# Products of blocks by sevens for queries, gates and outputs, in a hybrid of attention, feed-forward and state layers

## The chip, the cores and the metric

The kernel runs on one core of a Trainium2 chip. Times are device microseconds (us) of one execution. The engines are TensorE (PE: matmuls, with weight loads as PEld beside them), VectorE (DVE), ScalarE (ACT) and GpSimd (POOL), and SyncE (SP), whose queue issues nearly all DMAs. All data is f32.

## What is computed

Four layers stand one behind the other on a stream x of 4 batches, 1024 tokens and 256 features; each adds to x. The same feed-forward layer is used twice.

```
x = x + attention(layernorm(x))
x = x + ffn(layernorm(x))
x = x + state(layernorm(x))
x = x + ffn(layernorm(x))
```

Attention is causal, with one head of 256: Q, K and V are products of 256x256 weights with a bias. The feed-forward layer mixes each token with the one before it, and gives sigmoid(xr Wr) * (relu(xk Wk)^2 Wv). The state layer is, in the reference's words:

```python
xn = (x - mu) / jnp.sqrt(var + 1e-05) * ln_g + ln_b
xz = xn @ W_in.T + b_in
x_proj, z = jnp.split(xz, 2, axis=-1)
z = jax.nn.silu(z)
...
y = x_mean @ W_C.T + D_skip * x_proj
y = y * z
y = y @ W_out.T + b_out
return y + residual
```

Between these lines, x_proj is reduced to 16 states, and each state is convolved over time with its own decay. Three products matter here: the queries (in the kernel one product of xn with a merged weight wm, since Q and K are folded into one), the gates z, and the outputs y @ W_out.

## The kernel before

**Tiles.** The kernel works by halves j of a batch: 512 tokens (HALF) by 256 features. Activations are kept with features on the partitions, as two chunks c of 128 features by 512 tokens, or with tokens on the partitions, as four rows of 128 tokens by 256 features. The stream x stays on the core, tokens on the partitions. A product with features on the partitions is `project_columns` (L653 on): for one chunk e of 128 output features, two matmuls (c = 0, 1) of 128 x 512 that accumulate in one PSUM bank. A product with tokens on the partitions is `project_rows` (L667 on): for two rows of tokens, four matmuls of 128 x 256 into one bank, the tokens' columns as stationary weights. A matmul in f32 is two instructions on TensorE.

- `queries(j, e)` (L1163): `project_columns` of xa with wm, then one copy with the bias from PSUM, on ScalarE or VectorE.
- `state_gates(j, e)` (L1394): `project_columns` of xnT with the second half of w_in, then SiLU with the bias from PSUM on ScalarE.
- `state_outputs(j, g)` (L1570): `project_rows` of the gated z with w_out, then one VectorE add of 128 x 512 to x (L1577).

So each batch (two halves) has eight matmuls of 512 columns for queries, eight for gates, and sixteen of 256 columns for outputs.

**Memory.** All working tiles of the phases come from one pool of 34 equal slots. A new tile takes a slot that an older one has left, and its first writer waits until that one's last reader is done. PSUM has four single banks ("bank") and two pairs of banks ("pair"); scores and `skip` take pairs, the other products banks.

**Order.** The class `Order` (L49 on) records every step: a unit of TensorE with its cost, or an operation of another engine with one or more ways to do it (engine, cost), its needs, and what PSUM it frees. TensorE's units run in the order in which they were written down. `finish` (L162) works out by when each operation is due, and then goes through time with these costs: each engine takes the operation that can start first, and of those the one that is due first. What it chooses is written out as the fixed instruction order of each engine. `columns` (L41) is the cost of a unit's matmuls, `SHARE` and `MARGIN` (L65) say how much of its slack an operation may be held back.

**Phases.** The loop at L1627 is the attention phase: 32 score units (one for 128 queries), with the queries, values and feed-forward units of earlier halves between them (`mix_units`, L1590). After L1662 comes the last phase: the feed-forward units of halves 6 and 7, the gates, the reduction to states (`state_inputs`), the decay tables' loads (`load_decay`, sixteen DMAs of 512 KB, L1467), four convolutions (`convolve`, L1478), the exchange of their results through DRAM (`states_out`, L1498: four writes, L1503; `states_in`, L1515: four reads a batch, L1520), `skip(j)` (L1527: the product D_skip * x_proj, eight matmul instructions of 512 columns into a pair), `mix_states(b)` (L1541: it adds the states' part to the pairs of both halves, and VectorE gates z with them, L1556, four instructions a batch), the outputs, and `mix2`, the second feed-forward layer. `mix2.prepare(j)` makes a half's inputs: statistics on VectorE (L526, L527), a power on GpSimd (L543), normalization (L558, L564), a write and four reads through DRAM that turn it (L604, L610, with L616 on VectorE), and the mixture with the token before (L712 on ScalarE, L715 on VectorE). The feed-forward result is multiplied by its gate on VectorE (L791) and added to x on GpSimd (L797).

## Time and profile before

| | |
|---|---|
| median of three runs | 472.55 us (471.34, 472.55, 472.76) |
| the profiled execution | 471.39 us, its span 469.2 us |
| TensorE busy | 463.4 us (99%), 2074 matmul instructions |
| VectorE busy | 335.0 us (71%) |
| ScalarE busy | 190.6 us (41%) |
| GpSimd busy | 110.0 us (23%) |
| granted TensorE clock | 1.00 |
| moved by DMA | 69.42 MB, mean 148 GB/s |

The span runs from the first instruction of the program to the last; the execution's own time has some 2 us around it. A group's row in the profile names the line, the engine and the operation, then out<-in tiles and shapes, the count, the busy time and the mean of one in ns. A wait's row gives the total, the number of times and the longest. "SPq" rows are DMA issues; their durations are those of the issue, not of the transfer. A timeline row gives the start and the length of a run of equal instructions.

### The profile page before, as it was taken

The page shows a single profiled execution, that of the slowest core. Times are in us where ns is not written, and L with a number is a line of the kernel's source. Part 1 is how long each engine was busy: PE and PEld are TensorE (multiplying, and loading weights), DVE is VectorE, ACT ScalarE, POOL GpSimd, SP SyncE. Part 2 cuts the span into 40 slices and gives each one's busy share as a digit, 9 for nine tenths or more (in the row PEclk, how much of TensorE's full clock was granted, in tenths as well). Part 3 has the DMA queues.
Part 4 walks back from the last instruction along what each step waited for, and adds up shares of the span by engine and source line. Part 5 has one row for each costly group of instructions (what it writes and reads, how often), then busy time and mean ns, then how long its engine had stood idle before and what let it go on. Part 6 is the DMA issues. An engine that isn't in the chain of part 4 may idle for free.

```text
span 469.2 us, 6471 instructions
## 1 busy us (share of the span) xinstructions
PE 463.4 (99%) x2074; PEld 317.2 (68%) x2074; DVE 335.0 (71%) x886; ACT 190.6 (41%) x348; POOL 110.0 (23%) x119
## 2 busy tenths in 40 slices
PE   8999999999999999999999999999999999999996
PEld 5765775857867757866768756474565875877765
DVE  3678879589898897786897985411577984986642
ACT  3521333335235534537442585501113454345632
POOL 3000301112402503503322374300001310243330
PEclk9999999999999999999999999999999999999999
DMA  7047864844647854628883588903032241425312
GB/s 233 26 121 216 264 174 104 243 128 143 196 115 144 228 152 136 161 77 247 258 253 88 175 270 229 342 1 80 11 113 90 80 145 45 133 92 179 92 67 67
DMA packets 84914, 69.42 MB, mean 148 GB/s; under 512 B 20161, under 2 KB 82577, under 8 KB 84881
## 3 DMA queue, kind: packets, MB, share of 16 engines
q1 hardware_dynamic: 84064, 68.76, 49.7%
q8 instruction: 16, 0.26, 0.2%
q10 hardware_dynamic: 816, 0.26, 0.2%
q14 instruction: 18, 0.14, 0.1%
HBM read 40.54 MB, written 28.45 MB: 147 GB/s over the span
## 4 chain that ended last, share of the span: by engine, by line
PE 96%; DMA 1%; DVE 1%; ACT 0%; SPq 0%; issue 0%; DVEq 0%
PE sc L1217 13%; PE po L1322 13%; PE py L1534 6%; PE pv L1189 6%; PE pc L1484 2%; PE py L1546 1%; DMA wq<-in_L_attn_a_Wq_dram 1%; PE pb L1421 1%; PE pp_a0.pq L659 1%; PE pr_g1.pv L674 1%; PE pr_g0.pr L674 1%; PE pr_f4.pr L674 1%; PE pr_f3.pr L674 1%; PE pr_f2.pr L674 1%; PE pr_f1.pr L674 1%; PE pr_f0.pr L674 1%
## 5 line engine op out<-in xcount | busy, mean ns | idle before, releaser
L1322 PE MATMUL po<-v,prT 128*128 128x256 f32 x288 | 67.9, 380 | 0.4 <-DVE prT L1275 0.3
L1217 PE MATMUL sc<-xa,q 128*128 128x512 f32 (+3 forms) x192 | 67.0, 486 | 0.0
L1322 PEld LDWEIGHTS po<-v,prT 128*128 128x128 f32 x288 | 54.2, 190 | 11.1 <-issue 2.4
L1217 PEld LDWEIGHTS sc<-xa,q 128*128 128x128 f32 x192 | 35.2, 190 | 23.6 <-issue 18.7
L1238 ACT ACTIVATE pr<-pr,nmx 128x128 f32<-128x128 f32 (+7 forms) x32 | 24.7, 772 | 57.7 <-DVE pr L1233 55.5
L1189 PE MATMUL pv<-wv,xa 128*128 128x257 f32 x128 | 32.9, 380 | 0.0
L797 POOL TENSOR_TENSOR x<-x,r_g 128x512 f32<-128x512 f32 x14 | 20.1, 1432 | 51.7 <-DVE r_g L791 41.3
L543 POOL TENSOR_TENSOR rs_f<-ve_f,minus_half 128x4 f32<-128x4 f32 x8 | 8.3, 1037 | 99.3 <-DVE ve_f L530 99.3
L797 POOL TENSOR_TENSOR x<-x,r_f 128x512 f32<-128x512 f32 x16 | 20.3, 1271 | 42.9 <-DVE r_f L791 41.7
L1189 PEld LDWEIGHTS pv<-wv,xa 128*128 128x128 f32 x128 | 24.1, 191 | 7.8 <-issue 2.9
L1534 PE MATMUL py<-xnT,wk 128*128 128x512 f32 x64 | 28.8, 596 | 0.0
L1233 DVE TENSOR_SCALAR_CACHE_REDUCE pr<-sc,v 128x128 f32<-128x128 f32 (+7 forms) x32 | 26.2, 818 | 1.1
L1556 DVE SCALAR_TENSOR_TENSOR z<-py,b_skip,z 128x512 f32<-128x512 f32 x16 | 11.0, 742 | 22.2 <-PE py L1546 22.2
L1275 DVE STREAM_TRANSPOSE prT<-pblocks 128x384 f32<-128x384 f32 (+7 forms) x30 | 23.9, 797 | 3.2 <-DMA pblocks<-exps 3.0
L1332 DVE SCALAR_TENSOR_TENSOR x<-po,rsm,x 128x256 f32<-128x256 f32 x32 | 15.5, 484 | 12.4 <-PE po L1322 10.2
L543 POOL TENSOR_TENSOR rs_g<-ve_g,minus_half 128x4 f32<-128x4 f32 x8 | 8.6, 1078 | 58.3 <-DVE ve_g L530 55.8
L1366 POOL TENSOR_TENSOR x<-x,bout_r 128x512 f32<-128x512 f32 x16 | 20.4, 1286 | 8.1 <-ACT x L1359 8.0
L1534 PEld LDWEIGHTS py<-xnT,wk 128*128 128x128 f32 x64 | 12.0, 190 | 13.7 <-issue 13.0
L543 POOL TENSOR_TENSOR rs_h<-ve_h,minus_half 128x8 f32<-128x8 f32 x8 | 13.8, 1720 | 30.0 <-DVE ve_h L532 27.3
L1359 ACT ACTIVATE x<-x,mrs_h,rs 128x256 f32<-128x256 f32 x32 | 17.2, 590 | 2.9 <-DVE rsm L1331 2.9
L1199 DVE TENSOR_TENSOR v<-pv,bv_r 128x257 f32<-128x257 f32 x32 | 13.2, 414 | 6.9 <-PE pv L1189 6.6
L712 ACT ACTIVATE xk_g<-hT_g,muk 128x512 f32<-128x512 f32 x16 | 11.1, 715 | 16.6 <-DVE hT_g L616 16.6
(429 smaller groups left out, 949.9 us busy)
## 6 DMA issues: line engine op xcount, KB each, us to landing
hk<-r_dram SPq DMA_DIRECT2D x16, 512.0 KB, 8.3
rows_g<-xn_g SPq DMA_DIRECT2D x8, 512.0 KB, 3.1
blocks_g<-rows_g SPq DMA_DIRECT2D x32, 128.0 KB, 2.7
x<-in_L_attn_a_X_dram SPq DMA_DIRECT2D x7, 512.0 KB, 4.9
rows_f<-xn_f SPq DMA_DIRECT2D x7, 512.0 KB, 3.4
blocks_f<-rows_f SPq DMA_DIRECT2D x28, 128.0 KB, 2.8
rows_h<-xn_h SPq DMA_DIRECT2D x7, 512.0 KB
blocks_h<-rows_h SPq DMA_DIRECT2D x28, 128.0 KB, 3.5
```

The costliest lines, as they stand in the source:

```text
L543: nc.gpsimd.tensor_tensor(rs()[:, :k].rearrange("p k n -> p (k n)"), ve()[:, :k].rearrange("p k n -> p (k n)"), minus_half[:, : k * NH], A ...
L674: nc.tensor.matmul(pr()[:, j, :], lhsT=src()[:, c, ts(2 * g + j, P)], rhs=w[:, c, :], start=(c == 0), stop=(c == KC - 1),)
L797: nc.gpsimd.tensor_add(xg, xg, r()[:, ts(g, 2), :])
L1189: nc.tensor.matmul(pv()[:, : D + 1], lhsT=xaj()[:, c, ts(n, P)], rhs=wv[:, c, :], start=(c == 0), stop=(c == KC - 1),)
L1217: nc.tensor.matmul(sc()[:, k * HALF : k * HALF + w], lhsT=qh()[:, c, ts(n, P)], rhs=keys[k]()[:, c, :w], start=(c == 0), stop=(c == KC - 1),)
L1233: nc.vector.tensor_scalar(dst, src, v[2 * b + h]()[:, n, D : D + 1], None, ALU.add, ALU.min, accum_out=nmx(),)
L1238: nc.scalar.activation(p()[:, :nk], p()[:, :nk], AF.Exp, bias=nmx(), scale=-1.0, accum_out=sm())
L1275: nc.vector.transpose(dst()[:, : NH * width].rearrange("p (k m a) -> p k m a", m=NH, a=GRP), blocks().rearrange("p m (k a) -> p k m a", a= ...
L1322: nc.tensor.matmul(po()[:, :D], lhsT=src()[:, ts(n, P)], rhs=v[2 * b + n // NH]()[:, n % NH, :D], start=(n == 0), stop=(n == t),)
L1359: nc.scalar.activation(xt, xt, AF.Identity, bias=mrs()[:, 0, n : n + 1], scale=rs1()[:, n : n + 1])
L1366: nc.gpsimd.tensor_add(xg, xg, bout_r.unsqueeze(1).to_broadcast([P, 2, D]))
L1534: nc.tensor.matmul(dst()[:, ts(e, HALF)], lhsT=w_x[:, c, ts(e, P)], rhs=src()[:, c, :], start=(c == 0), stop=False,)
```

## The change

Queries of batches 2 and 3, gates of batches 1 to 3 and outputs of all four batches are computed for a whole batch at once, as a product of 2 x 2 blocks in seven products in place of eight (Winograd's form). The weight's blocks a(e, c) are 128 x 128; the stream's blocks b(c, h) are 128 features by the 512 tokens of half h. Four sums of weight blocks are made once on VectorE (`weight_sums`), four sums of stream blocks a batch on GpSimd or VectorE (`stream_sums`, tiles T0 and T1). Each of the seven products has a bank of its own, and its result is added by parts, mostly on VectorE. One scratch tile u is carried along. For gates, SiLU comes after that, on the tile itself.

For outputs (`seven_rows`) tokens are on the partitions: a product is four matmuls of 128 x 128. There are two scratch tiles, u and w. What belongs to one block alone is added from PSUM to x on VectorE, and the shared parts u and w on GpSimd (`grow`).

```diff
-    return 2 * k * max(n * 0.845e-3, 0.19)
+    return 2 * k * max(n * 0.845e-3, 0.105)
...
+    def weight_sums(t, a):
+        nc.vector.tensor_add(t[:, 0], a(1, 0), a(1, 1))
+        nc.vector.tensor_sub(t[:, 1], t[:, 0], a(0, 0))
+        nc.vector.tensor_sub(t[:, 2], a(0, 0), a(1, 0))
+        nc.vector.tensor_sub(t[:, 3], a(0, 1), t[:, 1])
...
+    def stream_sums(key, src, needs):
...
+        for k, plus, minus in (
+            (1, lambda: b(0, 1), lambda: b(0, 0)),
+            (3, lambda: b(1, 1), lambda: b(0, 1)),
+            (2, lambda: b(1, 1), lambda: sums(1)),
+            (4, lambda: b(1, 0), lambda: sums(2)),
+        ):
...
+                ("POOL", 1.05, partial(emit, nc.gpsimd)), ("DVE", dve(HALF), partial(emit, nc.vector)),
...
+    def seven_products(key, sums_key, a, s_of, src, t_of, out, bias, needs, there):
...
+        p = unit(1, lambda: a(0, 0), lambda: src(0)[:, 0, :], there)
+        o.op(f"{key}.u1", [f"{key}.p1"], *copies(u, p), frees="bank")
+        yield
+        p = unit(2, lambda: a(0, 1), lambda: src(0)[:, 1, :], there)
+        add("c11", 2, p, u, block(0, 0), 0, ["u1"])
+        yield
+        p = unit(6, lambda: s_of(2), lambda: t_of(2), [f"{sums_key}.T2"])
+        add("u2", 6, p, u, block(0, 1), None, ["u1"])
+        yield
+        p = unit(7, lambda: s_of(3), lambda: t_of(3), [f"{sums_key}.T3"])
+        add("u3", 7, p, block(0, 1), u, None, ["u2", "c11"])
+        yield
+        p = unit(4, lambda: a(1, 1), lambda: t_of(4), [f"{sums_key}.T4"])
+        add("c21", 4, p, u, block(1, 0), 1, ["u3"])
+        yield
+        p = unit(5, lambda: s_of(1), lambda: t_of(1), [f"{sums_key}.T1"])
+        add("c22", 5, p, u, block(1, 1), 1, ["u3"], last=False)
+        add("v12", 5, p, block(0, 1), block(0, 1), 0, ["u3"])
+        yield
+        p = unit(3, lambda: s_of(4), lambda: src(1)[:, 1, :], there)
+        add("c12", 3, p, block(0, 1), block(0, 1), None, ["v12"])
...
+    def seven_rows(key, sums_key, a, s_of, src, t_of, block, grown, needs, there):
...
+                for n in range(NH):
+                    nc.tensor.matmul(
+                        p()[:, n, :], lhsT=data()[:, ts(n, P)], rhs=wt(), start=True, stop=True
+                    )
...
+        def grow(name, e, h, more, need):
...
+                ("POOL", 1.3, lambda: nc.gpsimd.tensor_add(block(e, h), block(e, h), more())),
...
+        p = unit(2, lambda: a(0, 1), lambda: src(0)[:, 1, :], there)
+        add("v11", 2, p, to(0, 0), to(0, 0), grown(0))
+        grow("x11", 0, 0, u, k("u1", "v11"))
...
+        p = unit(5, lambda: s_of(1), lambda: t_of(1), [f"{sums_key}.T1"])
+        add("v22", 5, p, to(1, 1), to(1, 1), grown(1), last=False)
+        grow("x22", 1, 1, u, k("u3", "v22"))
+        add("w2", 5, p, w, w, k("u3", "v22"))
+        yield
+        p = unit(3, lambda: s_of(4), lambda: src(1)[:, 1, :], there)
+        add("w3", 3, p, w, w, k("w2"))
+        grow("x12", 0, 1, w, k("w3"))
```

The planner changes too. `finish` goes through time for 20 plans (five pairs of `SHARE` and `MARGIN`, four values of a new `WAIT`: an operation that is due sooner may be taken if it can start within `WAIT` of the first), and writes out the one whose end by its own costs is soonest. In the attention phase the queries' products are put one at a time between other units (`go_on`, at least 0.8 us of other units apart), the feed-forward units come two score units later, and two halves' inputs are prepared four score units sooner. The order of the last phase is new around the outputs:

```diff
-        j, k = divmod(i - 8, 4) if i < NI - 1 else (6, 0)
+        j, k = divmod(i - 10, 4)
...
     skip(1)
+    more_gates(4)
+    mix_states(0)
+    more_gates(4)
+    outputs = outputs_of_batch(0)
+    advance(outputs, 2)
+    skip(2)
+    advance(outputs, 2)
+    skip(3)
+    advance(outputs, 3)
+    prepare_batch(0)
+    mix_states(1)
     more_gates(3)
-    mix_states(0)
+    skip(4)
+    outputs = outputs_of_batch(1)
+    advance(outputs, 2)
+    skip(5)
+    advance(outputs, 5)
+    prepare_batch(1)
+    mix_states(2)
     more_gates(2)
-    outputs(0)
-    skip(2)
-    skip(3)
-    mix_states(1)
-    outputs(1)
-    outputs(2)
-    skip(4)
-    outputs(3)
-    skip(5)
     both(mix2.keys, 0)
-    mix_states(2)
     both(mix2.gates, 0)
+    outputs = outputs_of_batch(2)
+    advance(outputs, 2)
     both(mix2.values, 0)
-    outputs(4)
+    advance(outputs, 2)
     both(mix2.keys, 1)
-    outputs(5)
+    advance(outputs, 3)
+    prepare_batch(2)
     both(mix2.gates, 1)
     skip(6)
+    more_gates(2)
     both(mix2.keys, 2)
     skip(7)
     mix_states(3)
     both(mix2.values, 1)
-    outputs(6)
+    outputs = outputs_of_batch(3)
+    advance(outputs, 2)
     both(mix2.gates, 2)
-    outputs(7)
+    advance(outputs, 3)
     both(mix2.values, 2)
+    advance(outputs, 2)
+    prepare_batch(3)
```

There, `more_gates(n)` takes the next n gate units: whole matmul pairs for batch 0, and one of the seven products each for batches 1 to 3. `advance(outputs, n)` does n of the seven products of the outputs. `mix2.prepare` of both halves now follows the whole batch's outputs.

## Prediction

> **What bounds the kernel now.** I read the page's busy times and slices first, then TensorE's waits, then the costs of one matmul by shape, then the timeline of the exchange in the last phase. The page:
>
> ```profile
> span 469.2 us, 6471 instructions
> ...
> PE 463.4 (99%) x2074; PEld 317.2 (68%) x2074; DVE 335.0 (71%) x886; ACT 190.6 (41%) x348; POOL 110.0 (23%) x119
> ...
> DVE  3678879589898897786897985411577984986642
> ...
> PE 96%; DMA 1%; DVE 1%; ACT 0%; SPq 0%; issue 0%; DVEq 0%
> ```
>
> TensorE is busy 99% of the span, and the chain that ended last is 96% TensorE. A busy TensorE is not yet a TensorE without holes, so its own waits come next (us in total, times, longest):
>
> ```profile
> PE dust L1034 <- DVE idle L353: 1.2, 1, 1.2
> PE po L1322 <- DVE prT L1275: 0.3, 1, 0.3
> PE pt_wq_n L1045 <- DMA wq<-in_L_attn_a_Wq_dram: 0.2, 1, 0.2
> ```
>
> These are all of them: 1.7 us, nearly all before the first real matmul. So every matmul that goes is worth its full spacing, and every wait that the change makes is paid in full. VectorE is the second engine: in the slices it stands mostly at 7 to 9 tenths through the attention phase (90 to 290 us: 167.8 of 200 us busy), at 4, 1 and 1 tenths from 293 to 328 us, at 4 to 9 after that, and falls off at the end.
>
> **What one matmul costs.** The mean of one (592, 379, 275 ns) includes a tail of about 165 ns that the next one covers; the spacing is read from starts:
>
> ```profile
> 322.31 1.88 PE L659 MATMUL pp_pz0.6_2930<-xnT,w_in 128*128 128x512 f32 x4
> 324.02 1.88 PE L659 MATMUL pp_pz1.6_2939<-xnT,w_in 128*128 128x512 f32 x4
> ...
> 330.44 1.89 PE L674 MATMUL pr_pyo0.0_2966<-w_out,z 128*128 128x256 f32 x8
> 332.17 1.89 PE L674 MATMUL pr_pyo1.0_2971<-w_out,z 128*128 128x256 f32 x8
> ```
>
> An f32 matmul is two instructions ("passes"). Four passes of 512 columns take 324.02 - 322.31 = 1.71 us, 0.429 each; eight of 256 take 1.73, 0.216 each. For 128 columns with fresh weights each time, the last rows of the program:
>
> ```profile
> 463.90 1.49 PE L818 MATMUL pr_g7.last<-w_fv,ka_g 128*128 128x256 f32 x10
> 464.12 1.08 PEld L818 LDWEIGHTS pr_g7.last<-w_fv,ka_g 128*128 128x128 f32 x8
> ```
>
> The window holds two passes of 256 and eight of 128 columns: 1.49 - 0.165 - 2 x 0.216 = 0.893, so 0.112 each. Eight loads of 190 ns stand within 1.08 us: they start 0.13 apart and lie beside the matmuls.
>
> **The change, step by step.**
>
> *TensorE.* A batch's queries or gates are 8 matmuls of 512 columns before, 7 after: 2 x 0.429 = 0.86 us less. Queries change in two batches, gates in three: 5 x 0.86 = 4.3. Outputs are 32 passes of 256 columns a batch (6.91 us) and become 28 matmuls, 56 passes of 128 columns (6.27): 0.64 x 4 = 2.6. In the built programs' orders TensorE goes from 1088 to 1131 instructions, 48 - 5 more, which is this and nothing else. **Sum: -6.85 us.**
>
> The outputs' part hangs on the 128-column spacing. The row above says 0.112. [...] The row shows full-height loads beside matmuls, so I keep 0.112.
>
> *The exchange of states.* The convolutions' result goes to DRAM and back before the first product with it (mix_states(0), L1546):
>
> ```profile
> 317.05 3.70 PE L1534 MATMUL py<-xnT,wk 128*128 128x512 f32 x8
> ...
> 317.51 1.78 SPq L1503 DMA_DIRECT2D m_dram<-xm  x4
> ...
> 320.75 7.72 SPq L1520 DMA_DIRECT2D xmT<-m_dram  x12
> ...
> 325.83 1.14 PE L1546 MATMUL py<-xmT,w_c 16*128 16x512 f32 x8
> ```
>
> Twelve reads take 7.72 us to issue, so the fourth (the last of batch 0) goes out at 322.7; a read lands 2.6 us after its issue (2.6 to 3.5 over sixteen): 325.3. The cover is skip(1), 8 passes, and three gates, 12 passes: 8.6 us from 317.05, just enough. After, it is skip(1) and four single products, 16 passes: 6.86 us, TensorE ready at 323.9. **+1.4 us**; 0.5 if the writes land sooner, 2.3 with a landing of 3.5.
>
> *Decay tables and the slots.* The new tiles (two sums and one or two scratch tiles a batch) come from the same 34 slots. In the built program the load of hk_2_0, last of sixteen, gets the slot of xnT_0, whose last reader is skip(0); before, no load there reuses a slot freed less than some 14 us of matmuls earlier. From the end of skip(0) to convolve(2), which needs it, TensorE has four transposes (0.45), two products (1.72) and two convolutions (7.20 / 4 = 1.8 each): 5.8 us. These loads land 4.8 to 9.1 us after issue, median 8.3; plus 0.4 of issue that is 0.6 early at one end, 3.7 late at the other. The slow landings stand in the stretch where eight were issued in 4.69 us; this one goes out alone, so I take the short one: **0**, bounds 0 and +3.7.
>
> *VectorE.* An add of a product out of PSUM is L1577's instruction, 0.60 from start to start. Queries: 14 adds and 5 stream sums in two batches, against 8 copies of which ScalarE has most; some +10 us in 200 with 168 busy: 90%. I went along the two orders and compared, from each VectorE instruction that reads a product to each TensorE instruction that waits for VectorE, the work of both. In the kernel before, no stretch has more VectorE work than TensorE work. After, the attention phase's tightest is 21.4 against 21.6 us: **0**, bound +1.5. In 310 to 430 us VectorE has 78 us now and gets 28 adds of outputs less the 16 that go, 15 of gates and 10 sums and copies: 37 x 0.60 = 22, so 100 in 116. One place overflows: after mix_states(1) TensorE has three products (2.57 us) before skip(4), which needs the PSUM pair that two of L1556's instructions (0.66 each) free, and between these VectorE's order has three pairs of statistics (0.53 each) and a small one: 3.0 + 0.2 for the handover, 0.65 late. Two more places (the first product of outputs, the first keys of the last phase) come out even within 0.2. **+1.0** in all; bounds 0 and +2.5.
>
> *GpSimd.* It gets 16 adds to the stream and some 17 stream sums, about 43 us more at 1.27 us (L797's rows on GpSimd). Its own load is no matter (23%), but it and VectorE get in each other's way (duration min/median/max):
>
> ```profile
> L715 DVE SCALAR_TENSOR_TENSOR xk_f<-hT_f,muk,xk_f x16: 710/744/1772, 65.0 to 276.0; 128x512 f32<-128x512 f32 x16
> ...
> L715 DVE SCALAR_TENSOR_TENSOR xr_g<-hT_g,mur,xr_g x16: 718/746/1758, 352.8 to 449.6; 128x512 f32<-128x512 f32 x16
> ```
>
> A VectorE instruction with two operands in SBUF is 0.745 us alone and up to 1.77 beside a GpSimd add: 1.0 us more. The first keys of the last phase have 0.2 us to spare, and their xk is such an instruction beside the new stream adds. One collision there costs 0.8; I take **+0.5**, bounds 0 and +3 (four collisions at the batches' joints).
>
> *The rest.* Weight sums: 12 small VectorE instructions, where VectorE has air. SiLU stays 16 instructions on ScalarE (41% busy). The feed-forward units of the attention phase come later by two score units, which costs nothing as long as their inputs wait for them. The halves 5 and 7 of the stream are prepared four units sooner: statistics, and on SP one write and four reads each, ahead of exchanges of exponentials there; the DMA engines are 0.62 busy in that stretch and TensorE waited for prT once, 0.3 us. If an exchange comes late, one read's landing (2 to 3 us) is the price; I take nothing. The end (keys 3 to 7 of the last phase, 51 us of matmuls) stays in its order; all of it is prepared over 20 us ahead. The clock was granted in full (1.00) in every window.
>
> **The sum.** -6.85 + 1.4 + 1.0 + 0.5 = -3.95 us. The profiled execution took 471.39 us (span 469.2, 2.2 around it): 467.4. The runs' median is 472.55, 1.2 above it: 468.6 from there. I forecast the middle, 468.0.
>
> **Rivals.**
>
> 1. *All waits hidden.* Landings and joints come out at their lower bounds: -6.85 + 0.5, so 465.0 from the profiled run, 466.2 from the median. For it: TensorE had no hole before. Against it: the exchange had none to spare. Chance 0.18.
>
> 2. *The gain is lost to the decay table.* hk_2_0 lands after 8.3 us instead of 4.8, 2.9 late, and convolve(2) and all behind it wait: -3.95 + 2.9, about 471 us, no change. For it: the median of its own row. Against it: it goes out alone. Chance 0.13.
>
> 3. *VectorE becomes the bound* between mix_states(0) and the second keys of the last phase: slower. One third of some 34 GpSimd instructions there collide and cost 1.0 us each: VectorE's 100 us become 111 in 116, and at 96% each of the four batches' joints (first product, free pair, last add, xk) waits 2 us: 8 us, with the exchange -6.85 + 1.4 + 8 = +2.6: 475 us. It decides from joints of 1.4 us on. For it: 8 of 64 of L715's rows lie above 1.1 us. Against it: adds that read PSUM are not lengthened (L791 beside GpSimd: 0.68, as alone). Chance 0.11.
>
> 4. [...] Chance 0.02.
>
> **Chances and range.** The forecast and what lies near it (466.3 to 470.5) has 0.56; it and rival 1 are faster, with a little of rival 2. About 0.3% (1.4 us) is what a measurement here can tell from no change: faster than that 0.77, within it 0.12, slower 0.11. The range runs from rival 1 to the upper side of rival 2: 464.9 to 472.4.
>
> **What would show it.** TensorE's busy time some 7 us lower, L1812's passes (the outputs in the changed kernel) 0.112 apart. A wait of TensorE for xmT, 1 to 2 us; none for hk. Small waits for VectorE at skip(4) and before the first keys, under 1 us each. VectorE near 360 to 375 us busy, GpSimd near 155. The forecast is wrong if TensorE waits over 4 us in all, or if passes of 128 columns stand 0.15 us or more apart.

## The result, and the profile after

The changed kernel takes **485.98 us** (median of four runs, 481.53 to 487.64) against 471.94 for the kernel before (four runs beside it): a ratio of 1.028, with a 95% interval of 1.022 to 1.034. The forecast was 468.0, faster, in a range up to 472.4. The change is slower, and the forecast wrong in sign.

The profiled execution took 486.57 us. First its page, read as that of before: span, busy times, the slices of TensorE, VectorE, GpSimd and of the granted clock, and the chain that ended last.

```profile
span 484.8 us, 6802 instructions
...
PE 464.9 (96%) x2160; PEld 317.9 (66%) x2160; DVE 391.5 (81%) x948; ACT 195.5 (40%) x362; POOL 156.9 (32%) x155
...
PE   8999999999999989999996996999999999999996
...
DVE  4778779999699999899968978536589988999752
...
PEclk9999999999999999999998998899999999999999
...
PE 66%; DVE 18%; DMA 6%; SPq 3%; issue 3%; ACT 2%; POOL 1%; DVEq 0%; POOLq 0%
```

VectorE is at 391.5 us, where 360 to 375 were expected. TensorE's row has two holes, at 250 to 260 and 295 to 305 us, and behind each the clock row dips. The chain, 96% TensorE before, is 66% TensorE and 18% VectorE now. TensorE's own waits (us in total, times, longest) were 1.7 us before:

```profile
PE po L1477 <- DVE rsm L1486: 5.6, 1, 5.6
PE pt_h7.T L676 <- ACT xn_h L599: 2.1, 2, 2.0
PE pt_h7.T L676 <- DVE xn_h L593: 1.9, 2, 1.1
...
PE pp_g0.pk L694 <- DVE w_os L1822: 1.1, 1, 1.1
PE pr_g4.pv L801 <- ACT ka_g L883: 1.1, 1, 1.1
...
```

Releasers are inferred: the 5.6 us belong to the last product of attention weights and values, po_31, and what it waits for is the transposition of its weights (prT) on VectorE. The list leaves out waits that lie inside the recorded length of a matmul, as 2.0 us do in the first product with the exchanged states (further below). The next view is the stretches of 10 us in which the two holes begin (length; busy time of PE, PEld, DVE, ACT, POOL; granted clock; DMA share; GB/s).

```profile
250.00:260.00 10.00, 4.43 (x19) 3.58 (x18) 9.34 (x13) 4.16 (x8) 4.81 (x3) 0.94 0.40 88
290.00:300.00 10.00, 7.77 (x19) 3.13 (x17) 8.60 (x21) 5.59 (x10) 8.49 (x7) 0.99 0.91 277
```

In the first, TensorE works 4.43 us while VectorE works 9.34. The clock record has half clock for 3.41 us from 258.9 and for 6.83 us from 299.8, and nowhere else before the end.

**Where the time is.** From each matmul's start to the next one's, less its own spacing, TensorE loses about 22.4 us more than in the kernel before: 5.7 before po_31; 5.0 at the transposes of half 7; 4.1 in matmuls at half clock; 2.0 inside the first product with the exchanged states; 2.5 in the attention phase (92 to 183 us: 2.9, of which the kernel before has 0.4); 3.3 at three joints of the last phase (0.8 at skip(4), 1.3 at its first keys, 1.2 at later values); at the start it loses 0.3 less. The parts are rounded. 22.4 less the 6.85 saved is 15.6, which is the difference of the spans (484.8 - 469.2).

**The first hole on VectorE.** VectorE's rows ahead of po_31, then GpSimd's beside them (start, length, idle time before in brackets):

```profile
250.56 1.31 DVE L651 STREAM_TRANSPOSE hT_f<-blocks_f 128x512 f32<-128x512 f32 x2 [3.91 <-DMA blocks_f<-rows_f]
...
252.36 2.18 DVE L842 SCALAR_TENSOR_TENSOR xk_f<-hT_f,muk,xk_f 128x512 f32<-128x512 f32 x2
254.47 3.41 DVE L842 SCALAR_TENSOR_TENSOR xr_f<-hT_f,mur,xr_f 128x512 f32<-128x512 f32 x2
257.81 1.23 DVE L1430 STREAM_TRANSPOSE prT<-pblocks 128x1024 f32<-128x1024 f32 x1
```

```profile
252.52 1.48 POOL L882 TENSOR_TENSOR ka_f<-ka_f 128x512 f32<-128x512 f32 x1 [5.35 <-DVE ka_f L877]
253.96 3.38 POOL L1521 TENSOR_TENSOR x<-x,bout_r 128x512 f32<-128x512 f32 x2
```

The transposition for po_31 stands last in VectorE's order, behind the inputs of the feed-forward half 6. VectorE first waits 3.91 us for a transfer, then xk_f and xr_f take 2.18 and 3.41 us for two, where two alone take 1.40, beside GpSimd's product and its adds of the output bias.

**The second hole on VectorE.** The transposes of half 7 take xn_h, its normalized rows. These come from a chain: the last values product of half 7's feed-forward layer, r_f on VectorE, the add to x on GpSimd, statistics, a power, and xn_h. Rows of that chain in the kernel before, and then in the changed one:

```profile
288.44 0.69 DVE L791 SCALAR_TENSOR_TENSOR r_f<-r_f,pr_f7.pv 128x512 f32<-128x512 f32 x1 [1.04 <-PE pr_f7.pv L674]
...
296.17 1.05 DVE L558 TENSOR_SCALAR xn_h<-x,mv_h,rs_h 128x256 f32<-128x256 f32 x3
```

```profile
288.69 1.25 DVE L712 TENSOR_TENSOR o_sums<-o_sums,w_out 128x128 f32<-128x128 f32 x1
289.87 1.35 DVE L713 TENSOR_TENSOR o_sums<-w_out 128x128 f32<-128x128 f32 x1
...
291.41 0.68 DVE L918 SCALAR_TENSOR_TENSOR r_f<-r_f,pr_f7.pv 128x512 f32<-128x512 f32 x1
...
299.48 2.76 DVE L593 TENSOR_SCALAR xn_h<-x,mv_h,rs_h 128x256 f32<-128x256 f32 x2
```

From the end of that last product to the last xn_h it was 8.9 us before (288.3 to 297.2) and is 12.9 now (289.4 to 302.2). The four weight sums of the outputs (288.4 to 291.4) stand in VectorE's order ahead of the second r_f, two of them long beside GpSimd's adds, and xn_h is long beside the bias adds. Over that chain TensorE had five gate units before (8.58 us) and has four and one of the seven products now (7.72). So 4.0 us of this hole are a longer chain, and only 0.9 are matmuls that are gone.

**Theory.** VectorE has so little slack that its lengthening beside GpSimd's wide adds reaches TensorE, through chains with fixed order; the holes then bring on half clock. **Rivals:** GpSimd's own queue; the planner's choice of a plan; the later place of the feed-forward units; the sevens' load in one part alone; cover that the shorter products no longer give.

### The profile page after: what moved, and what is told of

It reads as the page before. It is cut to its first block, busy times and chain, and to the rows that moved or that the text cites. A ratio compares the mean times of both kernels' runs of the same rounds, so it can differ in the third digit from the quotient of the medians.

```text
span 484.8 us, 6802 instructions
## 1 busy us (share of the span) xinstructions
PE 464.9 (96%) x2160; PEld 317.9 (66%) x2160; DVE 391.5 (81%) x948; ACT 195.5 (40%) x362; POOL 156.9 (32%) x155
## 4 chain that ended last, share of the span: by engine, by line
PE 66%; DVE 18%; DMA 6%; SPq 3%; issue 3%; ACT 2%; POOL 1%; DVEq 0%; POOLq 0%
PE sc L1372 8%; PE po L1477 8%; PE py L1729 5%; PE p_os L1812 4%; PE pv L1344 3%; PE p_zs L750 3%; PE p_qs L750 2%; SPq L645 2%; DVE xr_f L842 2%; PE pc L1679 1%; DMA rows_f<-xn_f 1%; SPq L1425 1%; DMA blocks_f<-rows_f 1%; PE py L1741 1%; PE pb L1616 1%
## 5 line engine op out<-in xcount | busy, mean ns | idle before, releaser
L1477 PE MATMUL po<-v,prT 128*128 128x256 f32 x288 | 69.5, 387 | 6.1 <-DVE rsm L1486 5.6
L1477 PEld LDWEIGHTS po<-v,prT 128*128 128x128 f32 x288 | 55.2, 193 | 18.6 <-DVE rsm L1486 6.0
L578 POOL TENSOR_TENSOR rs_a<-ve_a,minus_half 128x4 f32<-128x4 f32 x7 | 7.2, 1023 | 66.7 <-DVE ve_a L565 65.9
L1521 POOL TENSOR_TENSOR x<-x,bout_r 128x512 f32<-128x512 f32 x16 | 22.0, 1386 | 16.8 <-ACT x L1514 12.6
L924 POOL TENSOR_TENSOR x<-x,r_g 128x512 f32<-128x512 f32 x14 | 18.1, 1302 | 14.8 <-DVE r_g L918 14.6
L1830 POOL TENSOR_TENSOR x<-x,u_os 128x512 f32<-128x512 f32 x12 | 16.4, 1372 | 18.9 <-DVE x L1822 18.0
L599 ACT ACTIVATE xn_g<-x,mrs_g,rs_g 128x256 f32<-128x256 f32 x19 | 10.5, 591 | 17.1 <-DVE mrs_g L587 17.0
```

What stands on the lines that cost most here:

```text
L578: nc.gpsimd.tensor_tensor(rs()[:, :k].rearrange("p k n -> p (k n)"), ve()[:, :k].rearrange("p k n -> p (k n)"), minus_half[:, : k * NH], A ...
L924: nc.gpsimd.tensor_add(xg, xg, r()[:, ts(g, 2), :])
L1477: nc.tensor.matmul(po()[:, :D], lhsT=src()[:, ts(n, P)], rhs=v[2 * b + n // NH]()[:, n % NH, :D], start=(n == 0), stop=(n == t),)
L1521: nc.gpsimd.tensor_add(xg, xg, bout_r.unsqueeze(1).to_broadcast([P, 2, D]))
```

## The experiments

Times are medians, ratios are against the kernel before on the same chip, with 95% intervals.

### Idle matmuls in the two holes

```diff
         def emit():
+            for _ in range(20 if i == NI - 1 else 0):
+                nc.tensor.matmul(po(), lhsT=idle[:, :P], rhs=idle, start=True, stop=True)
             for n in range(t + 1):
```

The same, fourteen times, ahead of the transposes of half 7.

> Twenty idle matmuls (0.215 us each) into po_31's bank just ahead of po_31's first product, fourteen ahead of the transposes of half 7; no engine's order changes but for them. Theory: the two holes of TensorE (5.7 us before po_31, 5.0 in four parts at the transposes) bring on the two stretches of half clock behind them (3.41 and 6.83 us), which cost half their length, 5.1 us. With the holes filled the clock stays at 1.00, the work behind the holes starts when it did, and the time is 486 - 5 = 481 (479.5 to 482.5). Rival: the clock falls for a reason outside of TensorE's own holes; then the mean clock stays at 0.989 and the time at 486.

Measured: 481.4 us, ratio 1.021 (1.018 to 1.024); 4.6 us less than the changed kernel, as the theory said. The slices of the clock in the profiled execution:

```profile
PEclk9999999999999999999999999999999999999999
```

In it no half clock is left until the last us; the other three executions have mean clocks of 0.995 to 1.00, against 0.982 to 0.993 in the changed kernel. So the holes bring on the slow clock, and it costs some 4 to 5 us beyond the holes themselves.

### GpSimd's bias adds made thin

```diff
-            nc.gpsimd.tensor_add(xg, xg, bout_r.unsqueeze(1).to_broadcast([P, 2, D]))
+            nc.gpsimd.tensor_add(xg[:, :, :8], xg[:, :, :8], bout_r[:, :8].unsqueeze(1).to_broadcast([P, 2, 8]))
```

> The adds of the output bias to the stream on GpSimd (L1521, 16 of 128x512) shrink to 8 of 256 features; the other features' bias is left out. Every engine's order stays the same. Theory: the holes are VectorE's in-order queue, lengthened by instructions that take turns with GpSimd: before po_31 xk_f and xr_f took 2.18 and 3.41 us for two where 1.40 is their time alone (2.8 us in all), before the transposes of half 7 xn_h took 2.76 where 0.8 is (1.9 us). The first hole falls from 5.7 to about 3, the second by 1 to 2 us, and with shorter holes some of the half clock goes: 479 to 483. Rival: VectorE's order alone, with late inputs of the feed-forward half 6 (the transfer of rows_f), makes the holes; then under 1 us goes: 485 to 486.

Measured: 475.42 us, ratio 1.009 (1.005 to 1.012); 10.6 us less than the changed kernel, more than the theory said. The first hole is gone, the second is 1.5 us (its chain takes 9.9 us instead of 12.9), and VectorE is busy 383.9 us instead of 391.5. Most of the first hole's cure came from further up: the transfer that VectorE waited for (rows_f) was issued at 237.6 instead of 241.0 us, while TensorE was only 0.6 us earlier there. VectorE's instructions ahead of it are shorter too: xr_f at 224 to 228 us takes 1.37 us for two instead of 2.39. GpSimd's queue became shorter too, so one more run was needed to tell the two apart.

### A power in place of each bias add

```diff
+            nc.gpsimd.tensor_tensor(xg[:, 0, :6], quarter[:, :6], minus_half[:, :6], ALU.pow)
```

> In place of each of the 16 adds of the output bias, GpSimd takes a power of 128x6 constants and writes them over six features of the stream (so the bias is left out and six features of every second row of tokens become 2): an instruction about as long (128x4 takes 1.02 us, 128x8 1.65 or more) that moves almost no data. Orders stay the same. Theory: what makes VectorE late is that its instructions with both operands in SBUF and GpSimd's wide adds take turns. Then this is like the thin adds: xr_f of half 6 takes 1.40 for two, the first hole goes, 474 to 478. Rival: it is GpSimd's own queue, the adds standing ahead of the stream adds and powers that VectorE waits for. Then GpSimd is as late as before and the time stays at 484 to 487.

Measured: 475.38 us, ratio 1.007 (1.005 to 1.010), as with the thin adds. GpSimd's busy time is 156.9 us, the same as in the changed kernel; VectorE's is 384.0, and the chain to half 7 takes 10.1 us.

The place of the first hole, on VectorE and then on GpSimd:

```profile
248.48 2.18 DVE L844 SCALAR_TENSOR_TENSOR xk_f<-hT_f,muk,xk_f 128x512 f32<-128x512 f32 x2
250.58 1.40 DVE L844 SCALAR_TENSOR_TENSOR xr_f<-hT_f,mur,xr_f 128x512 f32<-128x512 f32 x2
251.91 1.23 DVE L1432 STREAM_TRANSPOSE prT<-pblocks 128x1024 f32<-128x1024 f32 x1
```

```profile
248.63 1.48 POOL L884 TENSOR_TENSOR ka_f<-ka_f 128x512 f32<-128x512 f32 x1 [2.78 <-DVE ka_f L879]
250.07 3.10 POOL L1523 TENSOR_TENSOR x<-quarter,minus_half 128x6 f32<-128x6 f32 x2
```

GpSimd is busy for 3.10 us beside xr_f, and xr_f takes its 1.40; xk_f, beside the wide product L884, is still 2.18. So not GpSimd's time but its data are in the way: two xr_f take 3.41 us beside adds of 128x512 in the changed kernel and 1.40 beside powers of 128x6 here, and a power reads SBUF too. This lengthening of VectorE's instructions beside GpSimd's wide ones is what "turns" stands for here.

### The same thin adds in the kernel before

The same edit in the kernel before, with the same part of the bias left out.

> The kernel before with GpSimd's 16 bias adds shrunk to 8 of 256 features (the other features' bias left out), orders the same. Theory: GpSimd's adds lengthen VectorE's instructions in the kernel before too, but there VectorE has slack ahead of each product that needs it, so it costs TensorE nothing: 470.5 to 472, no difference. Rival: the adds cost the kernel before as much as the changed one, so that thin adds gain some 10 us of whatever kernel: 461 to 464.

Measured: 470.34 us against 471.41, ratio 0.9973 (0.9964 to 0.9983): 1.1 us, where the changed kernel gained 10.6. VectorE is busy 330.7 instead of 335.0. That is a little below the theory's 470.5 to 472 and far from the rival's. The turns are taken there as well, but TensorE hardly waits for them.

### Queries as before the change

```diff
-SEVEN_FROM = 2
+SEVEN_FROM = 4
```

> Queries of all batches as before the change, gates and outputs in sevens; halves 5 and 7 are prepared as early as before; the planner plans anew. Theory: the queries in sevens cost only the small waits at 172 to 183 us (2.1 us) and save 1.7, and the first hole, at 253 us, lies 50 us behind them and comes from the feed-forward inputs of half 6 that fall due there: it stays within 2 us of 5.7, the time stays within 3 us of 486. Rival: the load that the queries' adds put on VectorE in the attention phase (some 10 us) is what makes VectorE late at 253 us; then the first hole and its half clock go: 478 to 480.

Measured: 479.47 us, ratio 1.017 (1.015 to 1.020). The time is the rival's: the first hole falls from 5.7 to 0.6. The second stays (4.1 us). But this kernel was planned anew, and the runs below lose the first hole by a new plan alone; so this run doesn't tell the queries' load from the plan.

### Feed-forward units back at their old place

```diff
-        j, k = divmod(i - 10, 4)
+        j, k = divmod(i - 8, 4) if i < NI - 1 else (6, 0)
```

> The feed-forward units of the attention phase stand two score units earlier, as before the change, and so does the start of the last phase (gates of half 6, one plain gate, values of half 6, transposition of half 7, three plain gates); queries, gates and outputs stay in sevens; one product less before mix_states(0), which costs 0.9; the planner plans anew. Theory: the first hole is due to the place of half 6's inputs just ahead of po_31's transposition in VectorE's order, so it goes with its half clock (5.7 + 1.9): 486 - 7.6 + 0.9 = 479 (477 to 481.5). The second hole stays. Rival: the sevens' load on VectorE and GpSimd makes the hole, wherever the units stand: 485 to 488.

Measured: 492.66 us, ratio 1.045 (1.042 to 1.049): slower still, and both readings miss. The hole before po_31 is gone, but TensorE waits in many small places from 273 to 303 us, 4.5 us at the transposes, and 2.5 before the second keys of the last phase. So the old place, with a new plan and one product less ahead of mix_states(0), is no cure; what the place alone is worth isn't shown.

### One plan, as before the change

```diff
-    PLANS = [
-        (share, margin, wait, change)
...
-    ]
+    PLANS = [(0.2, 2.5, 0.0, 0.0)]
```

> The changed kernel with the one plan that the kernel before has (share 0.2, margin 2.5, no waiting for a more urgent operation) in place of the best of 20. Theory: the planner knows neither the lengthened instructions nor the clock, its 20 plans end within 5.1 us of each other by its own costs, and any of them has tight places where VectorE falls behind; holes in other places, 479 to 489, TensorE's waits above 8 us. Rival: the plan that was chosen is what put half 6's inputs ahead of the transposition for po_31, and with the old plan the change does what it was forecast to do: 468 to 472.

Measured: 482.14 us, ratio 1.022 (1.019 to 1.025): the theory. The hole before po_31 is gone under this plan as well; in its place are waits of 1.4, 1.2 and 1.7 us at 92, 159 and 261 us, and the transposes of half 7 still wait 3.6. The choice among plans is worth some 4 us, not the 18 between forecast and result.

### The bias folded into the outputs

```diff
-        o.op(f"{key}.u1", [f"{key}.p1"], *copies(u, p), frees="bank")
+        add("u1", 1, p, lambda: rows_of(bout_r[:, :P]), u, ["bin"])
...
+        o.op(
+            f"{key}.u4", k("u3") + ["bout_d"],
+            ("POOL", 1.3, lambda: nc.gpsimd.tensor_add(u(), u(), rows_of(bout_d))),
+        )
```

> The full computation with 12 of GpSimd's 16 bias adds gone: the output bias of the first feature block is added to the shared part u as it is taken from PSUM (VectorE, 4 instructions, none for ScalarE), the difference to the second block's by one GpSimd add of u in each batch. The planner plans anew. Theory: GpSimd's wide adds in the attention phase were what made VectorE late, so the two holes shrink as with the thin adds: 473 to 478, clock 0.996 or better. Rival: what the thin adds won came from orders that stayed the same by luck, or comes back at the batches' joints in the last phase where the four new adds and copies fall: 479 to 487.

Measured: 481.13 us, ratio 1.020 (1.017 to 1.022): the rival. The first hole is gone here too, but a wait of 3.3 us stands before the first keys of the last phase, and 3.1 at the transposes with 6.83 us of half clock behind it. The thin adds showed what the turns cost in one order; a new plan puts the tight places elsewhere.

### Two more products ahead of the exchange

```diff
-    more_gates(4)
+    more_gates(6)
     mix_states(0)
```

With the bias folded; the two products come from behind the first states' inputs, and the outputs' weight sums are made sooner.

> As the folded kernel, with two gates' products moved from behind the first states' inputs to ahead of mix_states(0), and the outputs' weight sums made 15 us sooner. Theory: the exchange of states costs 2.0 us in the changed kernel since TensorE comes 2 us too soon; with two products of 0.86 more ahead of it that falls to 0.3, and VectorE's four weight sums (1.3 us each beside GpSimd) no longer stand in the chain to the transposes of half 7: 2 to 3.5 us below the folded kernel, 470 to 475. Rival: the cover taken away behind the states' inputs is needed there, where TensorE then waits for the copies: the same as the folded kernel within 1 us.

Measured: 479.67 us, ratio 1.016 (1.013 to 1.019), 1.5 less than the folded kernel: short of the theory's 2 to 3.5, a little beyond the rival's 1. The exchange itself went as forecast: the product with the exchanged states, in the changed kernel and then here:

```profile
331.95 3.17 PE L1741 MATMUL py<-xmT,w_c 16*128 16x512 f32 x8
```

```profile
321.22 1.14 PE L1741 MATMUL py<-xmT,w_c 16*128 16x512 f32 x8
```

2.0 us of waiting inside its eight instructions are gone with 1.7 us more cover.

### Each part alone

Queries alone: `queries_of_batch` and the changed attention phase, with gates, outputs and the last phase of the kernel before.

> The changed kernel's attention phase (queries of batches 2 and 3 in sevens, feed-forward units two score units later), with gates and outputs as before and the last phase in the old order; one plan. Theory: 10 us more of VectorE in the attention phase, where it has 168 busy of 200, is enough for collisions to reach TensorE: 1.7 us saved, holes of 4 to 10 us with their half clock at 90 to 300 us: 474 to 481. Rival: the attention phase absorbs it and the loss comes from gates and outputs: 469 to 472.

Measured: 473.85 us, ratio 1.005 (1.003 to 1.007): 2.4 us slower, in single waits of 0.9 to 1.5 us at 92, 159, 182 and 262 us, and clock 1.00. Just below the theory's 474 to 481, above the rival's: the attention phase doesn't absorb the load, but loses little by it. Three of its four waits stand where the changed kernel with one plan has them; the hole of 5.7 us is in neither.

Outputs alone: `outputs_of_batch` in the last phase of the kernel before.

> Outputs of all batches in sevens, all else as in the kernel before, one plan, attention phase untouched. 2.6 us saved, the exchange as covered as before. Theory: the attention phase and the transposes of half 7 are without holes; the joints of the last phase (skip(4), first keys, later values) cost 1 to 3 us: 470 to 473, VectorE below 365 us. Rival: the 16 stream adds on GpSimd make VectorE the bound in the last phase: 475 or more, with waits of over 2 us before the keys of halves 0 to 2.

Measured: 485.5 us, ratio 1.030 (1.028 to 1.031). The rival's time. One wait carries over half of it, and 10.24 us of half clock begin in it; behind a second wait, of 3.1 us, there are 3.41 more:

```profile
PE pp_g0.pk L689 <- DVE xk_g L837: 8.6, 1, 8.6
```

A half's stream is ready only when five to seven of its batch's products are, and the first keys stood 13 us of matmuls behind that. So they were moved:

```diff
     prepare_batch(1)
+    skip(6)
+    outputs = outputs_of_batch(2)
+    advance(outputs, 7)
+    prepare_batch(2)
     both(mix2.keys, 0)
```

> Outputs of all batches in sevens, as in the run of the outputs alone, but the first keys of the last phase stand behind skip(6) and all products of batch 2: some 24 us of matmuls behind the last product that half 0 needs, in place of 13. Theory: the 8.6 us before those keys were the order, not VectorE's load: a half's stream is complete only when most of its batch's seven products are, so what follows has to come later; with that the waits are small: 469 to 472. Rival: VectorE is the bound between the first outputs and the second keys, so the wait turns up elsewhere in that stretch: 475 or more.

Measured: 480.38 us, ratio 1.019 (1.016 to 1.022): the rival. The 8.6 us are 1.2 and the half clock is gone from the profiled execution, so that wait was the order's, but from 370 to 450 us VectorE is busy 76.3 of 80, and TensorE waits in eight places for 0.3 to 1.5 us. In the kernel before, VectorE had 59.8 of 80 in the same part of the work (360 to 440).

Gates alone: ahead of the transposes of half 7 and of the exchange as long a cover as in the kernel before, three of the sevens' products less in two other places.

> Gates of batches 1 to 3 in sevens, all else as in the kernel before, one plan. 2.6 us saved. A whole gate unit counts as two of the sevens' products, and the cover is kept: ten such halves ahead of the transposes of half 7, six behind skip(1) ahead of mix_states(0), as before the change; what falls short is four instead of six at the transposes of the feed-forward half 7 and three instead of four behind mix_states(0). The stream sums of batch 3 are asked for just ahead of skip(1). Theory: without the queries' load and with the covers kept, the saving stays: 468 to 470.5. Rival: the stream sums on GpSimd lengthen the chain to the transposes of half 7, which waits 2 us or more and brings on half clock: 472 to 476.

Measured: 476.0 us, ratio 1.011 (1.007 to 1.014): the rival's number. TensorE waits 1.8 us in the feed-forward of half 7 and 2.7 at its transposes. Over the chain to those transposes it has 8.58 us of matmuls, as before the change, but the chain takes 12.4 us instead of 8.9: at this place it is the chain that grew, and not the cover that shrank.

### Cover put back ahead of the transposes of half 7

```diff
     more_gates(5)
+    skip(0)
     state_transpose(7)
...
-    skip(0)
+    more_gates(2)
     state_inputs_rows(1)
-    more_gates(2)
```

First in the changed kernel, else untouched:

> The changed kernel with one move: skip(0), 3.44 us of matmuls that need nothing of half 7, stands ahead of the transposes of half 7 instead of behind the states' inputs, and two gates' products take its old place. Theory: the stretch from po_31 to the transposes of half 7 is a chain of fixed length through VectorE, GpSimd and the DMA turn; the change took matmuls out of it (5 products of 7 where whole gates stood), so TensorE waits there. 3.44 us of other matmuls fill most of the second hole (5.0 us) and its half clock (3.4 us at least) goes: 486 - 3.4 - 2 to 3.4 = 479 to 481; the first hole stays. Rival: the hole is made by VectorE's lateness there, which moves with the order: 484 to 487.

Measured: 481.73 us, ratio 1.023 (1.020 to 1.026); the profiled execution took 478.69. The eight transposes in it run through without a wait:

```profile
295.25 1.04 PE L676 MATMUL pt_h7.T<-ident,xn_h 128*128 128x128 f32 x8
```

There are 11.15 us of matmuls over the chain now, and under the new plan it takes 10.8 us, with the outputs' weight sums no longer in it. So the hole can be filled from elsewhere; that lost cover had made it, the run doesn't show. (The new plan also made the first hole 0.8, and put 2.0 us before the second keys of the last phase, so the total says less than this place.) Then with the gates alone:

> Gates of batches 1 to 3 in sevens, all else as in the kernel before, skip(0) ahead of the transposes of half 7, three plain gates ahead of the keys of half 7 as before, one plan. 2.6 us saved. In the run of the gates alone TensorE waited 1.8 us at the feed-forward of half 7 (less cover) and 3.1 at the transposes. Theory: with the cover that the sevens took away put back from elsewhere, the saving stays: 468.5 to 471, faster than before or the same. Rival: stream sums on GpSimd and adds on VectorE lengthen the chain itself, TensorE waits on whatever covers it: 473 or more.

Measured: 472.38 us, ratio 1.003 (1.001 to 1.006), 3.6 less than gates alone; between the theory's range and the rival's. TensorE still waits 1.2 us at the transposes: the chain takes 12.4 us as in the gates alone, under 10.3 us of matmuls.

> As the run of the gates with skip(0) moved, but all stream sums are VectorE's. Theory: GpSimd's sums take as much from VectorE by turn-taking as they save, so the same or up to 2 us faster: 467.5 to 470.5. Rival: 12 more instructions of 0.68 us on VectorE in the chain to half 7 cost more: 1 us or more slower than with GpSimd.

Measured: 470.85 us, ratio 0.999 (0.997 to 1.001): no difference from the kernel before that can be told, 1.5 us less than with GpSimd's sums, as the theory said, and no wait at the transposes: without GpSimd's sums the chain takes 10.6 us. The last run of this kind, gates and outputs together:

> Gates as in the run of the gates alone and outputs as in the run with later keys; queries and the attention phase as before the change, one plan. 5.1 us saved. Theory: where every cover is as long as before and VectorE has slack, the saving is kept but for 1 to 3 us of joints: 467 to 470.5. Rival: in the last phase gates and outputs together fill VectorE (15 and 12 adds more, 17 sums), it falls behind at the joints, and no version with both is faster than before: 472 or more.

Measured: 480.97 us, ratio 1.020 (1.018 to 1.022): the rival.

> As the run with gates and outputs, but all stream sums are VectorE's (0.68 us each) and none GpSimd's (1.27 us, beside which an instruction of VectorE with SBUF operands is up to 1 us longer). Theory: a sum on GpSimd costs VectorE about as much by turn-taking as it would cost on VectorE, so this is within 1.5 us of the other, either way. Rival: GpSimd's sums are free help: 2 us or more slower.

Measured: 478.75 us, ratio 1.015 (1.013 to 1.017), 2.2 less with all sums on VectorE, a little beyond the 1.5 of the theory and against its rival: GpSimd's sums are no free help. No version of the change was measurably faster than the kernel before.

## Why the prediction was wrong

**TensorE, -6.85: right.** Sixteen passes of 128 columns of the outputs take 338.60 to 340.43, 0.114 each, with sixteen loads of 0.19 us beside them, within 1.86 us from 338.54; a product of the gates is 0.86 us.

```profile
338.60 2.00 PE L1812 MATMUL p_os<-w_out,z 128*128 128x128 f32 x16
340.43 2.74 PE L1729 MATMUL py<-xnT,wk 128*128 128x512 f32 x6
```

That is within 0.002 us of the last rows of the kernel before (0.112): the loads beside the matmuls add next to nothing to a pass.

**Exchange, +1.4: right in kind, 2.0 in size.** **Decay table, 0: right.** The convolutions take 7.19 us, 7.20 before, and wait for nothing.

**VectorE, +1.0: the step that failed**, at "the attention phase's tightest is 21.4 against 21.6 us: 0, bound +1.5", and with the weight sums, put at nothing ("where VectorE has air"). In the attention phase, measured are 2.9 us of small waits and the 5.7 of the first hole. The comparison set the work of VectorE, at its undisturbed durations, against TensorE's between a product and the instruction waiting for it. It left out chains that go out over a transfer and come back into VectorE's queue (po_31's transposition behind the inputs of half 6), and a margin of 0.2 us in 21 can't carry any lengthening. The joints of the last phase, 3.3 us, were forecast as 1.0: skip(4) at 0.65 (0.8 measured), the first keys as even (1.3), the later values not at all (1.2).

**The transposes of half 7: left out.** The sum has no term for this place, where TensorE works through a chain from half 7's last product to xn_h; the hole is 5.0 us. The chain grew from 8.9 to 12.9 us, by the four weight sums in it and by turns with GpSimd, and 0.86 us of matmuls went from over it. The thin adds, with every order kept, take 3.0 of those 4.0 us back. It was not a chain of fixed length, as the run that moved skip(0) took it to be. VectorE's air in the slices (4 tenths and less from 293 to 328 us) doesn't help there: what counts is what stands between the chain's own instructions.

**GpSimd, +0.5 with bounds 0 and +3: the mechanism was named, its size wrong by far.** It was priced as single collisions at the last phase's joints. But the lengthening adds up along a chain, and the adds that hurt most were old ones, 16 bias adds that cost the kernel before 1.1 us: the thin adds and the powers take 10.6 us off the changed kernel. It isn't only a sum: GpSimd's turns had to be there for the first hole, and so had the chosen plan, for in every kernel that was planned anew it is 0.8 us or less. Whether the queries' load had to be there isn't shown, since it went only with a new plan. VectorE was also busier than forecast (360 to 375 us) without these turns: 384.

**The clock, granted in full: read off the kernel before and carried over.** A trace without holes can't show what a hole does to the clock: 4.1 us in the changed kernel's matmuls at half clock, 4.6 by the run with idle matmuls.

**Rivals.** The third, VectorE as the bound through collisions, is what happened, but not where it was put: between mix_states(0) and the second keys no joint reaches the 1.4 us from which it was to decide. The holes lie in the attention phase and at half 7. It had 0.11, with one price of 475; the outputs alone, once moved, show VectorE as the bound of the last phase too (76.3 of 80 us).

What stays open: how the 14 us divide among queries, gates and outputs, and what the weight sums ahead of half 7 cost by themselves, since no run moved them alone. Alone, queries, gates and outputs cost 2.4, 4.5 and 14 (9 with later keys), but every version is planned anew, and its tight places move.

## What to carry to other kernels

When TensorE has no holes, saving its time by giving VectorE and GpSimd more work must be priced by their slack along every chain that comes back to TensorE, transfers included, with durations as they are beside the other engine; a chain with 0.2 us to spare counts as late. List each place where TensorE works through a chain of other engines, and compare both sides there: the matmuls over it, which the saving shortens (2.0 us at the exchange of states here), and the chain, which the new work lengthens (4.0 us at the transposes of half 7). Spread of load over GpSimd isn't free as long as its instructions are wide: 16 adds of 128x512 cost VectorE 7.6 us of busy time here.

## What the runs showed of the hardware

- **Half clock after a hole that is not all idle.** Thirteen of the sixteen stretches of half clock in the traces here follow a hole that the waits show (the run's end left out). They are 3.41, 6.83 and once 10.24 us long, and in the 3.41 us ahead of each TensorE had been busy between 0 and 1.98 us: 0.00 and 1.27 in the changed kernel, 1.98 (1.2 of them transposes) in the run with powers, where it waited 1.4 us at those transposes. The 2.7 us of waiting in the run of the gates alone brought on none in the profiled execution; its other three have mean clocks of 0.994 to 0.996. The changed kernel's four runs have mean clocks of 0.993, 0.989, 0.986 and 0.982.
- **A hole inside busy rows.** The other three stretches (thin adds, one plan, folded bias; 3.41 us each) follow the first product with the exchanged states. From its start to the next matmul's its eight matmuls take 2.7 us with the thin adds, and 1.07 in the kernel before: 1.6 us of waiting for the states (1.8 and 2.0 in the other two), which neither the list of waits nor the busy time shows, since a matmul's record of 0.6 to 0.7 us covers the wait for the next. In the changed kernel the same wait, 2.0 us, brought on no half clock in the profiled execution. The row with the thin adds, where half clock begins at 322.44 us:

```profile
319.33 2.79 PE L1741 MATMUL py<-xmT,w_c 16*128 16x512 f32 x8
```

- **Small instructions suffer as much as large ones.** A sum of 128x128 weights on VectorE takes 0.29 us with no add of GpSimd beside it and 1.26 beside GpSimd's adds, 0.96 more; xk_f of 128x512 took 0.74 us and up to 1.77 in the kernel before, 1.03 more:

```profile
L712 DVE TENSOR_TENSOR q_sums<-q_sums,wq x1: 291/291/291, 28.2 to 28.2; 128x128 f32<-128x128 f32 x1
L712 DVE TENSOR_TENSOR o_sums<-o_sums,w_out x1: 1255/1255/1255, 288.7 to 288.7; 128x128 f32<-128x128 f32 x1
```
